# An adaLN block on one core: the causal mask as rank-32 products on row tiles, gate logits in column tiles, result gathers held apart in the plan, and order edges for the shared port

## The chip, the core and the metric

The kernel runs on one core of a Trainium2 chip. The core has TensorE (PE; its weight loads are shown apart as PEld), VectorE (DVE), ScalarE (ACT), GpSimd (POOL) and SyncE (SP), each with its own queue of instructions that runs in order, and 16 DMA engines. Matrix products go from SBUF into PSUM, whose eight banks hold 512 fp32 values in each of 128 partitions. The metric is the device time of one launch in microseconds; smaller is better.

## The reference

The input x has 32 samples of 256 tokens and 128 features. The reference computes one transformer block whose shifts, scales and gates come from a conditioning vector c of each sample:

```
mod = silu(c) @ wmod                 # sa, ca, ga, sb, cb, gb of each sample
h = layernorm(x) * (1 + ca) + sa
x = x + ga * gated_linear_attention(h)        # 4 heads, chunks of 64 tokens, running state
h = layernorm(x) * (1 + cb) + sb
x = x + gb * ffn(h)
```

The part called ffn is itself an attention and a mixture of experts:

```
h = h + mla(rmsnorm(h))              # 16 heads of 8, keys and values from a latent of 64, rope,
                                     # causal mask, softmax, over the 256 tokens of a sample
logits = rmsnorm(h) @ gate_w.T + gate_b
e = argmax(logits)                   # one of 4 experts for each token
y = relu(rmsnorm(h) @ W1[e].T + b1[e]) @ W2[e].T + b2[e]
```

Its result is h + y.

## The kernel before

The work is done in 16 steps of two samples each, that is 512 tokens, or four tiles of 128 (`NT`). A step has four parts. `gla` is the gated linear attention. `front` makes queries, keys and values of the second attention. `core` is that attention itself. `gated` is the last norm and the choice of an expert. For steps 0 to 13, `route` then sorts the tokens by expert within groups of 3, 3, 3, 3 and 2 steps: rows are scattered into a table in DRAM (line 1366), `experts` fetches blocks of 128 rows of one expert, gathers that expert's weights (line 1381), computes the two products (lines 1397 and 1411) and stores the results (line 1419). `finish` gathers the results back, four gathers of 128 rows each step (line 1431), scales and adds them, and stores the output (line 1437). Steps 14 and 15 are not sorted: `dense` computes all four experts (lines 1274 and 1285) and keeps the chosen one.

**The order of instructions** is made by a planner in the kernel's own Python, the class `Plan`. The code above records operations, each with a key that says where in the whole it belongs. `Plan.run` is a list scheduler: it has a clock for each engine, takes a cost for each operation from `weigh` (or from a figure given with `together`), and takes the operation that can start first, within a window of 1.5 steps of keys. `either` records one operation with two or three engines to choose from. Operations of one `together` stay side by side. POOL operations, and DVE operations with two operands in SBUF or in a fast mode, are marked as users of a port that both engines share (`way[4]`, from `port`); the planner lets them not overlap, through the variable `shared`. `emit` then issues the instructions in the planned order. Planned times are not kept on the chip: an engine goes on as soon as its next instruction's inputs and buffers are there.

**Buffers.** PSUM is split into one tile of four banks (`sc`), used for scores, and four of one bank (`ps`). There is only one `sc`, so each use of it waits until the one before has been read out.

**Scores are computed twice in `core`.** `masked_scores` computes scores with queries in partitions, for the row maxima: for each of two samples three sets, one with four heads a bank and 128 keys, and two with two heads a bank and 256 keys, 96 sets in all. In each, every bank gets the causal mask first, by a full-array bf16 product of the identity with a mask of 0 and -2^120 (line 1025; four products of 512 or of 256 columns), and then the scores are added in 32-row tiles of the array (line 1032). DVE reduces the four banks to negated maxima (`nm`, line 1038). `probabilities` computes the scores again with keys in partitions, with the maxima put in by products with `sel` on 8 rows of each row tile (line 1076, bf16) and the scores in 32-row tiles (line 1082). ACT takes the exponential into `pT` (line 1088), POOL sets the masked part to zero (line 1091), and `values` multiplies by the values in 32-column tiles (line 1108).

**The gate** in `gated` multiplies four fp32 tiles of 128 tokens, as weights of the array, by a matrix of four columns (line 1193), and adds the bias on DVE (line 1198).

## Time and profile before

| | |
|---|---|
| median of 9 runs | 1179.47 us (1172.43 to 1184.82) |
| profiled execution, its own time | 1178.97 us |
| its span, first to last instruction | 1176.4 us |
| granted TensorE clock, mean | 0.962 |
| line 1025, mask products | 384, busy 73.5 us |
| line 1038, maxima on DVE | 96, busy 219.7 us |
| line 1193, gate products | 128, busy 16.1 us |
| line 1431, result gathers on POOL | 56, busy 56.7 us |

The profile is of one execution, which took 1178.97 us; its rows add up to its span of 1176.4 us. Busy time of an engine is the union of its instructions. TensorE's instructions overlap and their ends are modelled, so what a block of products costs is read from its first start to the start of the next block. The chain that ended last goes back from the last instruction, at each step to what released it or to the instruction before it on its engine, so its shares say where time would have to be saved. "Another core or an unknown queue", and "remote" in the timeline, mean that a wait ended with an event that the profile does not place. A fp32 product shows as two instructions.

### The profile page before, as it was taken

What the parts mean: (1) busy time and instruction counts of PE and PEld (TensorE: products, weight loads), DVE (VectorE), ACT (ScalarE), POOL (GpSimd) and SP (SyncE); (2) the same over time, 40 slices, a digit from 0 to 9 for tenths busy, and PEclk for the clock granted to TensorE, in tenths of its full rate; (3) what the DMA queues carried; (4) which work ended last, traced back from release to release, by engine and by line L of the source; (5) the groups of instructions that cost most, each with busy time, mean ns of one, the idle gap of its engine ahead of it and who ended that gap; (6) DMA issues with size and microseconds to landing.
All of it is one profiled execution on the core that took longest, in us unless ns stands there. A gap on an engine that the chain in (4) does not pass through costs nothing.

```text
span 1176.4 us, 27631 instructions
## 1 busy us (share of the span) xinstructions
PE 1038.1 (88%) x11109; PEld 685.2 (58%) x11109; DVE 839.5 (71%) x1888; ACT 749.0 (64%) x1522; POOL 522.5 (44%) x539
## 2 busy tenths in 40 slices
PE   4778889899979999988999989799899999878995
PEld 2444555555546666665666565366666666556774
DVE  4678688878968678686888787587878678633333
ACT  3766867676766777676685858377675757443441
POOL 7123324234464343766443554634254765422422
PEclk9789999999989999999999999999999999998998
DMA  4410011001122232233322232323422334334421
GB/s 122 120 36 10 15 37 35 24 20 32 35 82 65 87 97 87 86 104 93 104 69 70 91 116 80 85 96 88 151 69 89 107 100 135 91 93 142 149 67 48
DMA packets 76608, 94.96 MB, mean 81 GB/s; under 512 B 8560, under 2 KB 59552, under 8 KB 76224
## 3 DMA queue, kind: packets, MB, share of 16 engines
q0 software_dynamic: 15456, 52.44, 14.5%
q1 hardware_dynamic: 60416, 40.10, 11.6%
q8 instruction: 87, 1.43, 0.5%
q10 hardware_dynamic: 608, 0.66, 0.2%
q14 instruction: 41, 0.34, 0.1%
HBM read 74.94 MB, written 20.59 MB: 81 GB/s over the span
## 4 chain that ended last, share of the span: by engine, by line
PE 62%; DVE 16%; ACT 7%; issue 4%; POOL 2%; another core or an unknown queue 2%; DMA 1%; DVEq 0%; POOLq 0%; ACTq 0%
PE s L1032 8%; DVE nm L1038 8%; PE ao L1108 7%; PE t L1082 6%; PE s L1025 5%; PE y L1411 4%; PE h L1397 4%; ACT pT L1088 3%; PE o L880 2%; PE t L1076 2%; PE y L1285 2%; PE wo L908 2%; PE fo L1147 2%; PE h L1274 2%
## 5 line engine op out<-in xcount | busy, mean ns | idle before, releaser
L1038 DVE TENSOR_REDUCE nm<-s 128x8 f32<-128x2048 f32 (+1 forms) x96 | 219.7, 2289 | 58.4 <-PE s L1032 52.5
L1091 POOL TENSOR_SCALAR_AFFINE_SELECT pT<-pT 128x1024 f32<-128x1024 f32 (+1 forms) x96 | 135.7, 1413 | 215.7 <-ACT pT L1088 213.0
L1088 ACT ACTIVATE pT<-t 128x2048 f32<-128x2048 f32 x96 | 180.0, 1875 | 51.3 <-PE t L1082 47.7
L1381 POOL DMA_INDIRECT w<-wtab,widx x71 | 69.5, 978 | 176.3 <-DVE y L1416 54.2
L1032 PE MATMUL s<-akT,qm 32*128 32x256 f32 (+1 forms) x2048 | 118.5, 352 | 1.9 <-issue 1.7
L1108 PE MATMUL ao<-pT,vm 128*32 128x256 f32 (+1 forms) x2048 | 104.8, 332 | 8.2 <-issue 7.2
L1082 PE MATMUL t<-qm,akT 32*128 32x512 f32 x768 | 103.8, 612 | 0.5 <-issue 0.5
L1032 PEld LDWEIGHTS s<-akT,qm 32*128 32x128 f32 x2048 | 82.4, 190 | 33.0 <-issue 26.5
L1108 PEld LDWEIGHTS ao<-pT,vm 128*32 128x32 f32 x2048 | 59.8, 110 | 68.6 <-issue 36.7
L1406 ACT ACTIVATE ht<-h,w 128x128 f32<-128x128 f32 x183 | 57.2, 366 | 64.7 <-PE h L1397 38.1
L1025 PE MATMUL s<-mask,identb 128*128 128x256 bf16 (+1 forms) x384 | 73.5, 315 | 25.1 <-DVE nm L1038 23.1
L1397 PE MATMUL h<-xT,w 128*128 128x128 f32 x568 | 82.6, 293 | 9.6 <-ACT xT L1393 8.5
L1397 PEld LDWEIGHTS h<-xT,w 128*128 128x128 f32 x568 | 73.5, 201 | 21.5 <-ACT xT L1393 10.3
L1411 PE MATMUL y<-w,ht 128*128 128x128 f32 x568 | 80.2, 286 | 6.5 <-ACT ht L1406 5.6
L1411 PEld LDWEIGHTS y<-w,ht 128*128 128x128 f32 x568 | 70.3, 193 | 23.6 <-ACT ht L1406 10.7
L1025 PEld LDWEIGHTS <-identb 128*128 128x128 bf16 x384 | 37.0, 100 | 56.6 <-issue 44.9
L1431 POOL DMA_INDIRECT res<-ys,yidx x56 | 56.7, 1012 | 26.0 <-issue 15.1
L1366 POOL DMA_INDIRECT xs<-xm,yidx x56 | 58.2, 1040 | 11.5 <-issue 8.0
L1076 PE MATMUL t<-nmT,sel 8*128 8x256 bf16 (+1 forms) x1024 | 38.7, 245 | 15.1 <-ACT pT L1088 5.7
L868 POOL TENSOR_SCALAR_AFFINE_SELECT am<-am 128x2048 f32<-128x2048 f32 x16 | 32.2, 2011 | 42.5 <-ACT am L867 42.4
L1407 DVE TENSOR_SCALAR ht<-h,w 128x128 f32<-128x128 f32 x101 | 32.6, 346 | 25.5 <-PE h L1397 12.9
L1416 DVE TENSOR_TENSOR y<-y,w 128x128 f32<-128x128 f32 x71 | 20.3, 285 | 32.5 <-PE y L1411 21.2
(272 smaller groups left out, 2308.0 us busy)
## 6 DMA issues: line engine op xcount, KB each, us to landing
xb<-xs SPq DMA_DIRECT2D x71, 64.0 KB
ys<-y SPq DMA_DIRECT2D x71, 64.0 KB
x<-in_x SPq DMA_DIRECT2D x16, 256.0 KB
mod_b<-mod_d SPq DMA_DIRECT2D x16, 256.0 KB
mod_g<-mod_d SPq DMA_DIRECT2D x30, 128.0 KB
kept<-base SPq DMA_DIRECT2D x14, 256.0 KB
back<-kept SPq DMA_DIRECT2D x14, 256.0 KB
out<-res SPq DMA_DIRECT2D x14, 256.0 KB
```

What stands on the lines that cost most here:

```text
L1025: R.tensor.matmul(last, lhsT=identb, rhs=bc(mask, 1, per), start=True, stop=False, skip_group_check=True,)
L1032: R.tensor.matmul(banks[:, g, j * n_k * P : (j + 1) * n_k * P], lhsT=qm[r, j0 + j, t0 + qb * P : t0 + (qb + 1) * P], rhs=kT[r, t0 : t0 + n ...
L1038: R.vector.tensor_reduce(nm[b][:, qb, :, j0 : j0 + per], banks.rearrange("p g (a k) -> p g a k", a=per), AX.X, ALU.max, negate=True,)
L1076: R.tensor.matmul(banks[:, g, j * nq : (j + 1) * nq], lhsT=sel[r, j0 + j, :], rhs=nmT[r, q0:L], start=(j == 0), stop=False, skip_group_che ...
L1082: R.tensor.matmul(banks[:, g], lhsT=kT[r, t0 + kb * P : t0 + (kb + 1) * P], rhs=qm[r, j0 : j0 + per, t0 + q0 : t0 + L], start=False, stop= ...
L1088: R.scalar.activation(pT, banks, AF.Exp, scale=AD ** -0.5)
L1091: R.gpsimd.affine_select(part, part, [[0, 4 * per], [1, P]], ALU.is_ge, 0.0, base=0, channel_multiplier=-1)
L1108: R.tensor.matmul(o[32 * g : 32 * g + 32, h * L + q0 : (h + 1) * L], lhsT=vm[:, 2 * b + kb, hd, :], rhs=rhs, start=(h == 0 and kb == 0 and ...
L1366: indirect(lambda idx, src, pause: scatter(xs, idx, src, pause, puts), (idx, src, pause), (idx, src, *was), (t, pause), 3000,)
L1381: indirect(lambda w, idx: take(w, wtab, idx), (w, idx), (idx, *table), (w,), 4500)
L1397: R.tensor.matmul(h_ps[:, c * P : (c + 1) * P], lhsT=w[:, c * P : (c + 1) * P], rhs=xT, start=True, stop=True,)
L1411: R.tensor.matmul(y_ps[:, 0:P], lhsT=ht[:, c], rhs=w[:, FF + c * P : FF + (c + 1) * P], start=(c == 0), stop=(c == FC - 1),)
```

## The change

- **Mask.** The four full-array products of a set become sixteen of rank 32: the mask is kept as four blocks of 32 keys by 128 queries in each group of 32 partitions, and each block is multiplied by a 32x32 part of the identity, which writes 32 key columns of each head. Four row tiles write four banks side by side. The mask is now filled on POOL and not cast from a loaded constant.
- **Gate logits.** The gate matrix, padded to 32 columns, becomes the array's weights, and the four tiles of tokens go through four column tiles; the result is copied to SBUF, transposed on TensorE, and the bias is added from a strided view.
- **Planner.** Result gathers (`R.apart = 4000`) may start in the plan only 4 us after the one before. A POOL operation that is planned within 400 ns (`TURN`) of the last DVE user of the shared port gets a wait for that DVE instruction (`behind`, `add_manual_dep` in `emit`). Costs are changed: ACT with an accumulated output, `tensor_scalar` on POOL, `mm`, and three `together` figures. `normalise` no longer offers POOL.
- **Constants.** Two constants that served the mask or nothing are not loaded, and an unused mask is not computed. An unused helper, `urgent`, is gone (not shown below).

```diff
--- before.py
+++ after.py
@@ -98,7 +98,7 @@
 class Op:
     def __init__(self, key):
         self.key, self.ways, self.deps, self.helds, self.after = key, [], set(), [], []
-        self.soon = False
+        self.soon, self.apart, self.behind = False, 0, None
 
 
 class Hand:
@@ -120,7 +120,7 @@
         self.nc, self.tc, self.kinds = nc, tc, kinds
         self.ops, self.key, self.step = [], 0.0, 0.0
         self.joined = self.choice = None
-        self.soon = False
+        self.soon, self.apart = False, 0
         self.also = [], []
         self.tensor = Hand(self, "PE", nc.tensor)
         self.vector = Hand(self, "DVE", nc.vector)
@@ -130,6 +130,7 @@
 
     WAIT = {"PE": 300, "DVE": 300, "ACT": 300, "POOL": 0, "SP": 0}
     GAIN = 1.0
+    TURN = 400
 
     def at(self, start, span, ops):
 
@@ -233,9 +234,10 @@
         if engine == "PE":
             return 0, 170
         if engine == "ACT":
-            return 190 + n * 0.815 + 80 * pointers, 0
+            more = 190 if kw.get("accum_out") is not None else 0
+            return 190 + n * 0.815 + 80 * (pointers - (more > 0)) + more, 0
         if engine == "POOL":
-            return 190 + n * (0.9 if name == "affine_select" else 2.1), 0
+            return 190 + n * {"affine_select": 0.9, "tensor_scalar": 5.2}.get(name, 2.1), 0
         inside = any(
             isinstance(v, View) and v.held.kind in ("ps", "sc") for v in (*args, *kw.values())
         )
@@ -248,7 +250,7 @@
 
     def new(self):
         op = Op(self.key)
-        op.soon = self.soon
+        op.soon, op.apart = self.soon, self.apart
         self.key += self.step
         self.ops.append(op)
         return op
...
@@ -280,7 +275,8 @@
 
     def run(self, window):
         engines = {e: 0.0 for e in ENGINES}
-        shared = 0.0
+        shared = last = 0.0
+        holder = None
         nc, ops = self.nc, self.ops
         for n, op in enumerate(ops):
             op.n = n
@@ -342,6 +338,8 @@
                     t = max(engines[e], slot)
                     if way[4]:
                         t = max(t, shared - (150 if e == "DVE" else 0))
+                    if op.apart:
+                        t = max(t, last + op.apart)
                     for d in op.deps:
                         alike = d.engine == e and (e == "PE" or not d.land)
                         t = max(t, d.freed if alike else d.end + 60)
@@ -362,6 +360,13 @@
             engines[e] = t + way[1]
             if way[4]:
                 shared = max(shared, op.freed)
+
+                if e == "DVE":
+                    holder = op
+                elif holder is not None and holder.freed > t - self.TURN:
+                    op.behind, holder = holder, None
+            if op.apart:
+                last = t
             op.way = way
             order.append(op)
             done.add(op)
@@ -395,7 +400,12 @@
                         pool, full, *_ = self.kinds[h.kind]
                         h.real = pool.tile(list(full), F32, tag=h.kind, name=h.name)
                 with self.nc.source_location(__file__, line):
-                    call(*(now(x) for x in args), **{k: now(x) for k, x in kw.items()})
+                    op.made = call(*(now(x) for x in args), **{k: now(x) for k, x in kw.items()})
+            if op.behind is not None and op.behind not in op.deps:
+                self.tc.add_manual_dep(
+                    op.made.ins, op.behind.made.ins.name,
+                    mybir.DependencyInfo(mybir.DependencyClass.Sync, mybir.DependencyReason.SCHED_ONLY),
+                )
 
 
 def bc(ap, at, n):
@@ -445,11 +455,11 @@
     cT = load("cT", [P, B], R.sync, -9.0)
     R.at(-8.9, 0.02, 1)
     R.scalar.dma_start(wmod[:, 0 : 2 * P], d["wmod"][:, 0 : 2 * P])
-    cs = keep([P, 1028], "w_consts")
-    ident, bd, tri = cs[:, 0:128], cs[:, 128:384], cs[:, 384:512]
-    cos, sin, jm = cs[:, 512:768], cs[:, 768:1024], cs[:, 1024:1028]
+    cs = keep([P, 644], "w_consts")
+    ident = cs[:, 0:128]
+    cos, sin, jm = cs[:, 128:384], cs[:, 384:640], cs[:, 640:644]
     for at, end, src, key, eng in (
-        (0, 128, 0, -8.8, R.gpsimd), (128, 512, 512, -7.0, R.gpsimd), (512, 1028, 1408, -4.0, R.sync)
+        (0, 128, 0, -8.8, R.gpsimd), (128, 644, 1408, -4.0, R.sync)
     ):
         R.at(key, 0.0, 1)
         eng.dma_start(cs[:, at:end], d["consts"][:, src : src + end - at])
@@ -482,7 +492,10 @@
     for k in range(2):
         R.gpsimd.dma_start(f_wk[k * LAT : (k + 1) * LAT, :], d["f_wk"][:, k, :])
         R.gpsimd.dma_start(f_wv[k * LAT : (k + 1) * LAT, :], d["f_wv"])
-    gw = load("gw", [P, NE], R.gpsimd, -3.0)
+    R.at(-3.0, 0.001, 1)
+    gw = keep([P, 32], "w_gw")
+    R.gpsimd.memset(gw, 0.0)
+    R.gpsimd.dma_start(gw[:, 0:NE], d["gw"])
     R.at(-3.0, 0.0, 1)
     gbb = keep([P, NE], "gbb")
     R.gpsimd.dma_start(gbb, d["gb"].partition_broadcast(P))
@@ -521,12 +534,6 @@
     eps6 = filled([P, 1], "eps6", 1e-6, -9.0)
     one = filled([P, 1], "one", 1.0, -9.0)
 
-    cmask = keep([P, P], "cmask")
-    R.at(-6.9, 0.001, 1)
-    R.vector.tensor_scalar(cmask, tri, 0.0, None, ALU.is_ge)
-    R.vector.tensor_sub(cmask, cmask, ident)
-    R.vector.tensor_scalar(cmask, cmask, -1.0, 1.0, ALU.mult, ALU.add)
-
     headsum = keep([P, P], "headsum")
     R.at(-5.5, 0.001, 1)
     R.gpsimd.memset(headsum, 0.0)
@@ -549,8 +556,14 @@
     R.at(-4.0, 0.001, 1)
     identb = keep([P, P], "identb", BF16)
     R.vector.tensor_copy(identb, ident)
-    mask = keep([P, P], "mask", BF16)
-    R.vector.tensor_copy(mask, tri)
+
+
+    mask = filled([P, 4, P], "mask", 0.0, -3.5, BF16)
+    for g in range(4):
+        part = mask[g * 32 : g * 32 + 32]
+        R.gpsimd.affine_select(
+            part, part, [[-32, 4], [1, P]], ALU.is_ge, NEG, base=0, channel_multiplier=-1
+        )
 
     R.at(-3.5, 0.001, 1)
     selc = keep([P, 4], "selc")
@@ -582,7 +595,7 @@
 
 
     def mm(n, cols):
-        return n * (2 * max(112, 0.85 * cols) + 8)
+        return n * (2 * max(116, 0.88 * cols) + 8)
 
     def mm4(n, cols):
         return n * 2 * max(140, 1.04 * cols)
@@ -616,8 +629,6 @@
             with R.either():
                 R.vector.tensor_scalar(to, of, mean, rs, ALU.subtract, ALU.mult)
                 R.scalar.activation(to, of, AF.Identity, bias=nb[:, i : i + 1], scale=rs)
-                if times == 1:
-                    R.gpsimd.tensor_scalar(to, of, mean, rs, ALU.subtract, ALU.mult)
 
     def rms_normalise(dst, src, name):
         sq = R.tile("small", [P, P], f"sq{name}")
@@ -872,7 +883,7 @@
         oT = [R.tile("mid", [P, T], f"oT{s}_{c}") for c in range(2)]
         for c in range(2):
             o = ps(f"o{s}_{c}")
-            with R.together(1.05 * mm(6, P)):
+            with R.together(1.15 * mm(6, P)):
                 for n in range(NT):
                     b, i = n // 2, n % 2
                     for k in range(2):
@@ -1018,14 +1029,18 @@
 
             n_k, t0 = qb + 1, b * L
             banks = sc(f"s{s}_{b}{qb}{j0}")
-            with R.together(mm4(per, n_k * P) + mmb(4, per * P)):
-
-                for g in range(4):
-                    last = banks[:, g].rearrange("p (a c k) -> p a c k", a=per, c=n_k)[:, :, qb, :]
-                    R.tensor.matmul(
-                        last, lhsT=identb, rhs=bc(mask, 1, per), start=True, stop=False,
-                        skip_group_check=True,
-                    )
+            with R.together(mm4(per, n_k * P) + 16 * (3 + 4 * per)):
+
+
+                for c in range(4):
+                    for g in range(4):
+                        r = slice(g * 32, g * 32 + 32)
+                        last = banks[:, g].rearrange("p (a c k) -> p a c k", a=per, c=n_k)
+                        R.tensor.matmul(
+                            last[:, :, qb, c * 32 : c * 32 + 32], lhsT=mask[r, c, :],
+                            rhs=bc(identb[r, r], 1, per), start=(c == 0), stop=False,
+                            skip_group_check=True,
+                        )
                 for j in range(per):
                     for g in range(4):
                         r = slice(g * 32, g * 32 + 32)
@@ -1187,16 +1202,24 @@
         with R.either():
             R.scalar.activation(xT, pt, AF.Copy, scale=n2w)
             R.vector.tensor_scalar(xT, pt, n2w, None, ALU.mult)
-        g_ps = ps(f"gate{s}")
-        with R.together(mm(4, NE)):
+
+        t_ps = ps(f"gt{s}")[:, 0:P]
+        with R.together(280):
             for i in range(NT):
                 R.tensor.matmul(
-                    g_ps[:, i * NE : (i + 1) * NE], lhsT=xT[:, i * P : (i + 1) * P], rhs=gw,
+                    t_ps[32 * i : 32 * i + 32, :], lhsT=gw, rhs=xT[:, i * P : (i + 1) * P],
                     start=True, stop=True,
                 )
+        gt = R.tile("small", [P, P], f"gt{s}")
+        with R.either():
+            R.scalar.copy(gt, t_ps)
+            R.vector.tensor_copy(gt, t_ps)
+        g_ps = ps(f"gate{s}")[:, 0:P]
+        with R.together(130):
+            R.tensor.transpose(g_ps, gt, ident)
         lg = R.tile("tiny", [P, NT, NE], f"lg{s}")
         R.vector.tensor_add(
-            lg, g_ps[:, 0 : NT * NE].rearrange("p (i e) -> p i e", i=NT), bc(gbb, 1, NT)
+            lg, g_ps.rearrange("p (i e) -> p i e", i=NT)[:, :, 0:NE], bc(gbb, 1, NT)
         )
         mx = R.tile("tiny", [P, NT], f"mx{s}")
         R.vector.tensor_reduce(mx, lg, AX.X, ALU.max)
@@ -1307,9 +1330,10 @@
         for was in puts:
             tc.declare_no_dep(now.ins, was.ins, reason="places differ")
         puts.append(now)
+        return now
 
     def take(out, table, idx):
-        nc.gpsimd.indirect_dma_start(
+        return nc.gpsimd.indirect_dma_start(
             out=out, out_offset=None, in_=table[:],
             in_offset=bass.IndirectOffsetOnAxis(ap=idx, axis=0),
         )
@@ -1385,7 +1409,7 @@
             with R.with_tokens(reads=g["filled"], writes=(t,)):
                 R.sync.dma_start(x, g["rows"]["xs"][b * P : (b + 1) * P, :])
             pt = ps(f"xt{s}_{b}")
-            with R.together(110):
+            with R.together(180):
                 R.tensor.transpose(pt[:, 0:P], x, ident)
             xT = R.tile("small", [P, P], f"xT{s}_{b}")
             with R.either():
@@ -1426,11 +1450,13 @@
         with R.with_tokens(reads=(state[s]["keeps"],)):
             R.sync.dma_start(base.rearrange("p i f -> p (i f)"), state[s]["kept"])
         res = R.tile("mid", [P, NT, P], f"res{s}")
+        R.apart = 4000
         for i in range(NT):
             at, row = g["yidx"][:, s - g["first"], i : i + 1], res[:, i, :]
             indirect(
                 lambda row, at: take(row, g["ys"], at), (row, at), (at, *g["stored"]), (row,), 3500
             )
+        R.apart = 0
         resv = res.rearrange("p (b i) f -> p b i f", b=2)
         mul(resv, resv, bc(gb, 2, 2))
         add(res, res, base)
```

More of the change, by code (lines that the diff above doesn't have):

```diff
@@ L266, in urgent @@
     @contextmanager
-    def urgent(self):
-        self.soon = True
-        yield
-        self.soon = False
-    @contextmanager
     def either(self):
```

## The prediction

> **What bounds the kernel now.** I read the page's totals first, then the chain that ended last, then groups with shapes kept apart, TensorE's timeline, and the timeline around the longest holes of the chain.
>
> ```profile
> span 1176.4 us, 27631 instructions
> PE 1038.1 (88%) x11109; PEld 685.2 (58%) x11109; DVE 839.5 (71%) x1888; ACT 749.0 (64%) x1522; POOL 522.5 (44%) x539
> PE 62%; DVE 16%; ACT 7%; issue 4%; POOL 2%; another core or an unknown queue 2%; DMA 1%; DVEq 0%; POOLq 0%; ACTq 0%
> PE s L1032 8%; DVE nm L1038 8%; PE ao L1108 7%; PE t L1082 6%; PE s L1025 5%; PE y L1411 4%; PE h L1397 4%; ACT pT L1088 3%; PE o L880 2%; PE t L1076 2%; PE y L1285 2%; PE wo L908 2%; PE fo L1147 2%; PE h L1274 2%
> ```
>
> TensorE is busy for 88% and carries 62% of the chain; DVE comes next with 16%, half of it the reduction nm, which frees the single four-bank score tile. So work taken off TensorE should count, if nothing else takes its place. The windows show the middle (busy us of PE, PEld, DVE, ACT, POOL, then granted clock):
>
> ```profile
> 400.00:500.00 100.00, 96.37 (x1126) 65.00 (x1125) 75.28 (x185) 73.57 (x147) 47.66 (x48) 1.00 0.28 88
> 541.00:565.00 24.00, 20.41 (x178) 14.06 (x171) 15.72 (x33) 11.91 (x26) 20.49 (x20) 0.79 0.36 95
> ```
>
> From 400 to 500 TensorE is the limit (96 of 100 us). Around 541, where twelve gathers of line 1431 stand almost back to back, its clock falls to 0.79. Now the blocks that the change rewrites, in TensorE's timeline (start, length, xcount):
>
> ```profile
> 235.14 0.40 PE L1076 MATMUL t<-nmT,sel 8*128 8x128 bf16 x16
> 235.38 1.08 PE L1082 MATMUL t<-qm,akT 32*128 32x512 f32 x8
> 249.54 1.02 PE L1025 MATMUL s<-mask,identb 128*128 128x512 bf16 x4
> 250.50 1.17 PE L1032 MATMUL s<-akT,qm 32*128 32x128 f32 x32
> 258.95 0.60 PE L1025 MATMUL s<-mask,identb 128*128 128x256 bf16 x4
> 259.48 1.15 PE L1032 MATMUL s<-akT,qm 32*128 32x256 f32 x16
> ```
>
> From the start of one block to the start of the next is what TensorE pays. The medians over the run: mask with 512 columns 957 ns, with 256 columns 528 ns; sixteen products on four row tiles with 128 columns each (line 1076, the nearest thing to the new mask) 234 ns.
>
> The last reading is the holes, first in the chain, then in the timeline at the end of the second one:
>
> ```profile
> 1115.95 4.31 another core or an unknown queue
> 1145.83 9.53 another core or an unknown queue
> ```
> ```profile
> 1150.70 0.95 POOL L1431 DMA_INDIRECT res<-ys,yidx  x1 [0.30 <-issue]
> 1151.96 0.94 POOL L1431 DMA_INDIRECT res<-ys,yidx  x1 [0.30 <-issue]
> 1155.34 0.69 DVE L1290 TENSOR_TENSOR ye<-y,b 128x512 f32<-128x512 f32 x1 [9.51 <-remote]
> 1155.38 1.84 ACT L1279 ACTIVATE ht<-h,w_cols 128x512 f32<-128x512 f32 x3 [9.82 <-remote]
> ```
>
> DVE and ACT both stop for over 9 us with their inputs ready, while POOL issues gathers, and both go on soon after the last. All five packs of result gathers (from 541, 745, 933, 1107 and 1138 us) have such a hole within or just after them. What it waits for the profile doesn't name.
>
> **The change part by part.**
>
> *Mask.* Each of 96 score sets loses four full-array products and gains sixteen of rank 32. Removed: 32 x 957 + 64 x 528 ns = 64.4 us, of which the chain holds 4.6%, 54 us; the rest lies under waits for the score tile. Added, 512-column sets: sixteen products of 128 columns, as line 1076, 234 ns. The 256-column sets: sixteen of 64 columns, not in the trace: between half of that (117, if columns rule) and all of it (234, if the instruction rules); no row is nearer to one end, so I take 175. Added: 32 x 234 + 64 x 175 = 18.7 us, saving 45.7 (41.9 to 49.5). On the chain: 54 x 45.7/64.4 = 38.3 us.
>
> [...] Line 1076 starts sixteen in 234 ns, 14.6 ns apart. [...]
>
> *Gate logits.* Sixteen blocks of 914 ns (median, line 1193) go. In their place come four fp32 products in four column tiles, 128 columns, eight instructions: line 1108 with 128 columns runs sixteen such in 551 ns, so 276; then a transpose, a quarter of line 637's 437 to 530, about 120. TensorE saves 519 ns x 16 = 8.3 us; the chain's pieces at line 1193 sum to 9.9 us, so 5.6 there. Added: one 128x128 copy out of PSUM, 0.34 to 0.37 us as lines 1392 and 1393, 16 x 0.35 = 5.6 us on ACT or DVE, and a second bank for a moment. Ranks aren't needed until a group ends, and the last dense step has its choice at 1132 and uses it at 1142; without that cover it would be about 1 us once.
>
> *What of the 43.9 us stays.* What is late next is the score tile: the 2.29 us reduction and two handovers between sets remain, and TensorE already waits 23.1 us for it in total at line 1025. But the mask is itself part of that cycle, so the cycle shortens too. Ends: half stays (22), or all (44); TensorE's 92 to 96% in most of the middle is nearer to all, so three quarters: 33 us.
>
> *Gathers.* Their start in the plan is held 4 us apart; nothing on the chip holds them, only what the plan puts between them in POOL's queue. In the middle POOL has 356 other instructions in 1176 us, one each 3.3 us, many waiting for ACT, so the spread is real there. The holes, with what the granted clock in the windows around them takes: at 552.8, 2.4 us, and a clock of 0.79 over 24 us (5.0); at 758 to 761, 2.0, and 0.84 over 21 (3.4); at 952.6, 3.6; at 1116, 4.3, and 0.91 over 18 (1.6): 22.3 us. Ends 0 and 22.3; I take half, 11, as line 1366's scatters and line 1381's weight gathers stay as dense. The pack of 1138 has almost nothing else on POOL: I leave its 12.9 us (9.5, and 0.86 over 24) as they are. And 12 gathers 4 us apart take 44 us where dense work ends 33 us after the first: in the plan three of them come after the last product of acc on POOL (1171.5 in the trace), and in its in-order queue they would wait for that: three issues of 1.25, 2.5 to landing from the last, 1.4 for product and sum, against the one sum now: about +6, half as likely as not, +3. On SP the stores of line 1437 wait for these rows; loads of x and of expert rows stand behind them there. Net -8.
>
> *Order edges.* A POOL instruction planned within 400 ns of a DVE one that uses the shared port now waits for it. Behind it in POOL's queue stand the selects on pT and am (PE waits at lines 1108 and 880), scatters and gathers. Gain: DVE's sum at line 643 takes 1237 ns in the mean for sig and 690 to 693 where undisturbed; over lines 643, 648 and 773 I count some 24 us of such stretching, at DVE's 16% of the chain 4 us. Loss: nothing where POOL's idle 56% takes it; 10 us if an eighth of the 112 selects (14) pass one DVE sum of 0.7 us on to TensorE. Between -4 and +10 I take 0.
>
> *The rest.* 25 normalisations (0.85 us) leave POOL for DVE or ACT at 0.36 to 0.48, some 10 us over two engines with room. Unloaded constants and three mask instructions of 0.2 us on DVE at 8 us lie under the wait for the modulation weights (to 9.7 us); the new mask's fills on POOL, five instructions of at most 1 us each by line 868's rate, come before 84 us, when line 1025 first runs, and after them POOL is free. All zero. Other costs of the planner only reorder.
>
> Sum: -33 - 8 = -41 us. The profiled execution took 1178.97 us (span 1176.4 and 2.6 around it), 0.5 below the median 1179.47: 1138.
>
> **The rivals.**
>
> 1. *All of it counts.* TensorE's 44 us, 22 of holes and 8 of the last pack's 12.9: 1179 - 74 = 1105. For it: 88% busy. Against: 38% of the chain is not PE.
> 2. *Spread on paper only.* POOL runs ahead of the plan, packs stay, the last three gathers come late: 1179 - 33 + 6 = 1152. For it: no wait enforces the 4 us.
> 3. *The score tile takes over.* Reduction and exponential (2.29 and 1.88 us) set the pace; half of the 44, the gathers late: 1179 - 22 + 6 = 1163. For it: nm is 8% of the chain; against: DVE has a quarter free.
> 4. *Slower: edges hold the selects.* A select that waits for a DVE stuck behind a reduction passes 2.29 us to line 1108. It decides from 41/2.29 = 18 of 112 selects on; at 27 it gives 1200. For it: POOL's order is now tied to a DVE running late at places; against: POOL is 2% of the chain.
> 5. *No difference*, 1179: products that don't overlap at 64 columns.
>
> **How the numbers follow.** Forecast 0.43 (1122 to 1150), rival 1 0.16, 2 0.17, 3 0.11, 4 0.09, 5 0.04. A measurement here tells about 0.5%, 6 us. Faster: 0.87; same 0.04; slower 0.09. From 1100 to 1170 leaves out rivals 4, 5 and a third of rival 1, 0.18: low end from full gains (1097), high end from rival 3 with some edges.
>
> **What would show it.** Right: mask blocks of about 230 and 180 ns to the next start, TensorE's busy time near 985 us, gate blocks under 0.4 us; PE still first in the chain; clock above 0.8 where the result gathers run. [...]

## The result and the profile after

The changed kernel took 1204.64 us (median of 20 runs, 1196.41 to 1212.19) against 1178.04 for the kernel before (62 runs): a ratio of 1.0226, 95% interval 1.0205 to 1.0247. It is slower by 27 us, where 41 us less was forecast. The profiled execution took 1199.23 us.

The page of the changed kernel, its span, totals and the group of the new mask (line, engine, operation, tiles, count | busy, mean ns | idle before, by whom ended):

```profile
span 1197.0 us, 30027 instructions
PE 1008.7 (84%) x12277; PEld 671.6 (56%) x12277; DVE 842.1 (70%) x1907; ACT 758.1 (63%) x1548; POOL 491.2 (41%) x511
L1039 PE MATMUL s<-identb,mask 32*128 32x64 bf16 (+1 forms) x1536 | 35.0, 204 | 46.3 <-DVE nm L1053 40.1
```

TensorE's busy time fell by 29.4 us (from 1038.1), but the span grew by 20.6, so TensorE's idle time (span less busy) grew by 50: from 138.3 to 188.3. The waits of TensorE in the changed kernel (us in total, times, longest) say part of it; the first was 23.1 us before:

```profile
PE s L1039 <- DVE nm L1053: 40.1, 30, 6.2
PE t L1091 <- DVE nm L1053: 11.7, 10, 1.8
...
PE s L1047 <- issue: 8.0, 24, 0.9
...
PE s L1039 <- issue: 6.1, 9, 1.3
```

Two things are new: a wait of 6.2 us for the reduction nm (it takes 2.29 us, and the longest wait for it was 2.4 before), and 14.1 us of waits put down to nothing (issue) inside the blocks of the mask and the scores, where lines 1025 and 1032 had 2.2 before. A place that shows the second, in the timeline of the changed kernel (start, length, engine, line, operation; in brackets the idle time before it and what ended it):

```profile
551.35 0.98 POOL L1456 DMA_INDIRECT res<-ys,yidx  x1 [1.95 <-DVE qm L979]
552.65 0.96 POOL L1405 DMA_INDIRECT w<-wtab,widx  x1 [0.32 <-DVE y L1440]
553.91 0.95 POOL L1456 DMA_INDIRECT res<-ys,yidx  x1 [0.30 <-issue]
555.16 0.95 POOL L1456 DMA_INDIRECT res<-ys,yidx  x1 [0.30 <-issue]
556.42 0.95 POOL L1456 DMA_INDIRECT res<-ys,yidx  x1 [0.30 <-issue]
...
555.02 0.34 PE L1039 MATMUL s<-identb,mask 32*128 32x128 bf16 x9
555.65 0.28 PE L1039 MATMUL s<-identb,mask 32*128 32x128 bf16 x5 [0.29 <-issue]
557.07 0.23 PE L1039 MATMUL s<-identb,mask 32*128 32x128 bf16 x2 [1.14 <-issue]
...
558.56 0.01 DVE L1133 LOAD_MASK_SELECT sums<-ao  x1 [3.51 <-remote]
558.56 0.73 DVE L1133 STREAM_SHUFFLE sums<-ao 128x512 f32<-128x512 f32 x1
558.63 0.67 ACT L1016 COPY vm<-v 128x256 f32<-128x256 f32 x2 [5.96 <-remote]
```

From 555.05 to 558.56 DVE, ACT and TensorE stand still or crawl together, with their inputs ready (ACT's 5.96 us begin with 2.4 us of ordinary waiting for a product that ends at 555.1). I call this a stop. The wait of 6.2 us has one too: at 980.6 us DVE stops for 4.2 us ahead of nm, in a pack of four indirect DMAs, while ACT goes on, and TensorE waits for it from 980.9. (A pack is a row of indirect DMAs that POOL issues one straight after the other.) Sixteen products that elsewhere take 0.23 us to the next block take over 2 us here. The result gathers, meant to be 4 us apart, run 1.25 us apart. The windows of the changed kernel (length, busy of PE, PEld, DVE, ACT, POOL, then granted clock) show that the clock got better around one pack of gathers (0.79 before, over the same window) and worse around another (1.00 before, from 933 to 956):

```profile
541.00:565.00 24.00, 21.64 (x241) 14.48 (x238) 15.86 (x37) 14.19 (x26) 10.37 (x11) 0.93 0.30 87
975.00:990.00 15.00, 8.77 (x137) 7.13 (x127) 8.79 (x15) 7.74 (x33) 7.09 (x7) 0.76 0.47 131
```

Over the run, time at less than 0.9 of the clock rose from 92.5 to 158.7 us (the records of both profiles are at 1.0 or at 0.5, so I call it half clock too; the last of the profile's clock records runs 2 to 3 us past the span in both). The last reading is POOL's timeline at the end:

```profile
1177.72 1.42 POOL L658 TENSOR_TENSOR ye<-ye,oh 128x512 f32<-128x512 f32 x1 [13.11 <-DVE ye L1313]
1180.36 0.96 POOL L658 TENSOR_TENSOR acc<-acc,mod_g 128x256 f32<-128x256 f32 x1 [1.23 <-DVE acc L654]
1181.48 0.98 POOL L1456 DMA_INDIRECT res<-ys,yidx  x1 [0.16 <-issue]
...
1189.24 0.95 POOL L1456 DMA_INDIRECT res<-ys,yidx  x1 [0.30 <-issue]
```

Seven of the last twelve gathers stand behind the last product of acc. Dense work is done by 1182; the span ends at 1197.0. So several things that speak against the forecast are there: gathers 1.25 us apart, gathers after the last acc, and longer waits for nm.

### The profile page after: what moved, and what is told of

Its sections match the earlier page's. It is cut to its first block, busy times and chain, and to the rows that moved or that the text cites. A ratio compares the mean times of both kernels' runs of the same rounds, so it can differ in the third digit from the quotient of the medians.

```text
span 1197.0 us, 30027 instructions
## 1 busy us (share of the span) xinstructions
PE 1008.7 (84%) x12277; PEld 671.6 (56%) x12277; DVE 842.1 (70%) x1907; ACT 758.1 (63%) x1548; POOL 491.2 (41%) x511
## 5 line engine op out<-in xcount | busy, mean ns | idle before, releaser
L1047 PE MATMUL s<-akT,qm 32*128 32x256 f32 (+1 forms) x2048 | 127.1, 360 | 8.4 <-issue 8.0
L1123 PE MATMUL ao<-pT,vm 128*32 128x256 f32 (+1 forms) x2048 | 97.6, 332 | 5.9 <-DVE y L1440 2.4
L1047 PEld LDWEIGHTS s<-akT,qm 32*128 32x128 f32 x2048 | 89.5, 202 | 16.0 <-issue 13.2
L1421 PE MATMUL h<-xT,w 128*128 128x128 f32 x568 | 85.5, 299 | 10.4 <-DVE xT L1416 3.9
L1421 PEld LDWEIGHTS h<-xT,w 128*128 128x128 f32 x568 | 76.4, 208 | 23.6 <-issue 7.0
L1039 PE MATMUL s<-identb,mask 32*128 32x64 bf16 (+1 forms) x1536 | 35.0, 204 | 46.3 <-DVE nm L1053 40.1
L1431 DVE TENSOR_SCALAR ht<-h,w 128x128 f32<-128x128 f32 x112 | 36.3, 347 | 52.6 <-PE h L1421 23.3
L1039 PEld LDWEIGHTS <-mask 32*128 32x128 bf16 x1536 | 22.6, 94 | 85.3 <-issue 70.8
L913 DVE SCALAR_TENSOR_TENSOR oT<-o,w_cols,ro 128x512 f32<-128x512 f32 x32 | 23.9, 746 | 32.4 <-ACT ro L912 29.7
L653 POOL TENSOR_TENSOR sig<-sig,glow 128x512 f32<-128x512 f32 x12 | 15.2, 1270 | 75.4 <-ACT sig L861 47.6
```

Source lines behind the costliest of these rows:

```text
L1039: R.tensor.matmul(last[:, :, qb, c * 32 : c * 32 + 32], lhsT=mask[r, c, :], rhs=bc(identb[r, r], 1, per), start=(c == 0), stop=False, skip ...
L1047: R.tensor.matmul(banks[:, g, j * n_k * P : (j + 1) * n_k * P], lhsT=qm[r, j0 + j, t0 + qb * P : t0 + (qb + 1) * P], rhs=kT[r, t0 : t0 + n ...
L1123: R.tensor.matmul(o[32 * g : 32 * g + 32, h * L + q0 : (h + 1) * L], lhsT=vm[:, 2 * b + kb, hd, :], rhs=rhs, start=(h == 0 and kb == 0 and ...
L1421: R.tensor.matmul(h_ps[:, c * P : (c + 1) * P], lhsT=w[:, c * P : (c + 1) * P], rhs=xT, start=True, stop=True,)
```

## The experiments

Every comparison ran on one chip, but they were not all the same chip: I call that of the result A, those of the first and second comparison B and C, that of the third and fourth D. The kernel before took 1178.04 us on A, 1140.79 on B, 1144.13 on C, 1178.39 and 1175.79 on D. Traces of A and D have stops, mostly at the same places for the same kernel: of those of the changed kernel on A, its trace on D lacks the ones that end at 785 and 1137 us and some of DVE's. No trace of B or C has one. Nothing here tells whether A and D are one chip, nor parts the chip from the time of a comparison; D showed stops in both of its comparisons. Ratios are always to the kernel before in the same comparison; a ratio can differ by some tenths of a per cent from that of the two medians (e13: 0.9897, and 1167.87/1175.79 is 0.9933). Stops are counted as idle stretches over 0.7 us of ACT and of DVE, added up, for which the profile names nothing but "remote". So a stop of both counts twice, and ordinary waiting ahead of a stop is in it, as the 2.4 us above.

| kernel (all but the ratio in us) | chip | ratio | span | TensorE busy | idle | clock < 0.9 | stops |
|---|---|---|---|---|---|---|---|
| before | A | 1 | 1176.4 | 1038.1 | 138.3 | 92.5 | 68.5 |
| after | A | 1.0226 | 1197.0 | 1008.7 | 188.3 | 158.7 | 66.8 |
| e3, order of before | B | 1.0012 | 1144.6 | 1028.1 | 116.5 | 88.4 | 0 |
| e1, mask in it | B | 0.9736 | 1109.6 | 974.2 | 135.4 | 68.9 | 0 |
| e5, after | C | 0.9936 | 1131.1 | 973.0 | 158.1 | 101.1 | 0 |
| e8, mask and gate, new plan | C | 1.012 | 1154.6 | 990.2 | 164.4 | 122.4 | 0 |
| e9, after | D | 1.0162 | 1194.1 | 1005.6 | 188.5 | 156.7 | 44.8 |
| e13, mask, old order | D | 0.9897 | 1169.1 | 1011.8 | 157.3 | 129.1 | 64.8 |
| e12, the same with edges | D | 0.981 | 1147.4 | 999.2 | 148.2 | 98.6 | 62.5 |
| e16, before, new plan | D | 1.023 | 1208.0 | 1046.4 | 161.7 | 116.1 | 61.4 |
| e14, after with pauses | D | 1.0215 | 1206.3 | 1004.5 | 201.8 | 164.0 | 2.6 |

**First: which part? (chip B)**

e1: the mask's products of the change in the kernel before; the planner is told the old figure, so every other instruction keeps its place on its engine.

```diff
             with R.together(mm4(per, n_k * P) + mmb(4, per * P)):
-                for g in range(4):
-                    ... lhsT=identb, rhs=bc(mask, 1, per) ...
+                for c in range(4):
+                    for g in range(4):
+                        ... lhsT=mask[r, c, :], rhs=bc(identb[r, r], 1, per) ...
```

> The kernel before with one thing changed: the mask of the first scores as sixteen rank-32 products a set. The planner still charges the old figure, so every engine's order is that of before; TensorE has some 45 us less work. Three theories. Score tile: what TensorE saves at the mask turns into waiting for nm and into half clock, since everything else keeps its pace; 1170 to 1182 us. Order: the mask is worth what it was priced at (33 us) and the loss of the whole change comes from the new plan; 1140 to 1155 us. Order edges: as the order theory for this run, since it has no edges.

Measured: 1112.32 us, 0.9736 (0.9678 to 0.9795). As a ratio this is the order theory's range (1140 to 1155 us are 0.968 to 0.980 of A's 1178). The groups of e3's mask (first fence, the old products) and of e1's (second), shapes apart:

```profile
L1036 PE MATMUL s<-mask,identb 128*128 128x256 bf16 x256 | 39.3, 277 | 16.7 <-DVE nm L1049 16.3
L1036 PE MATMUL s<-mask,identb 128*128 128x512 bf16 x128 | 34.2, 391 | 1.5 <-ACT pT L1099 1.1 <-DVE nm L1049 0.4
```
```profile
L1040 PE MATMUL s<-identb,mask 32*128 32x64 bf16 x1024 | 19.1, 191 | 25.2 <-DVE nm L1054 24.9
L1040 PE MATMUL s<-identb,mask 32*128 32x128 bf16 x512 | 13.5, 225 | 2.8 <-DVE nm L1054 1.7 <-ACT pT L1104 1.1
```

The kernel before has no trace on B; e3 (below) has its order, and took 1.0012 of its time, so it stands in for it. TensorE's busy time falls by 53.9 us, the span by 35.0; 18.9 come back as idle time, 9.9 of them as waits for nm in these groups (26.6 against 16.7). e3's profiled execution was its slowest, 4 us over its median, so 35.0 is a little high. So the mask does what was forecast, when nothing else moves.

e2 and e3: the order edges alone, taken from the changed kernel in e2 (its order kept), and added by the same rule to the kernel before in e3 (about a hundred waits in its order).

```diff
-            if op.behind is not None and op.behind not in op.deps:
-                self.tc.add_manual_dep(
-                    op.made.ins, op.behind.made.ins.name, ...)
```

> The changed kernel in its own order, without the waits of POOL instructions for DVE instructions (about 100 of them). Order edges theory: these hold POOL's selects and gathers behind a late DVE and cost 20 us or more; 1175 to 1185 us. Score tile and order theories: they lie in POOL's idle time; 1198 to 1208 us.

> The kernel before in its own order, with such waits added by the same rule (about 100). Order edges theory: 1195 to 1205 us. The other two: within 6 us of before, 1172 to 1184 us.

Measured: e2 1.0046 (1.001 to 1.0081), e3 1.0012 (0.9984 to 1.0041). The edges cost nothing in the old order. e2's ratio lies where the edges theory had it (1175 to 1185 us were 0.997 to 1.006 of 1178), far below the 1.0226 of A. That this is the chip and not the edges shows only in e5 below: with the edges, the changed kernel took 0.9936 on C, where there are no stops either, so without them it is no faster. With that, edges that hold POOL are out as the cause.

e4: the changed kernel without the 4 us, planned anew.

```diff
-        R.apart = 4000
+        R.apart = 0
```

> The changed kernel with the result gathers planned without the 4 us between them (a new plan). If the spread makes the end later (three gathers behind the last dense product) or blocks POOL, this is 8 to 20 us faster than the changed kernel, 1184 to 1196 us. Score tile theory: within 6 us of the changed kernel. Order theory: any plan may come out some 1% to either side, so 1190 to 1215 us.

Measured: 0.9937 (0.9903 to 0.9971). That is a little faster than before, below every range I gave, which were all taken from A. Beside e5's 0.9936 (on C) it makes no difference.

**Second: the changed kernel elsewhere, and its tail (chip C)**

e5 is the changed kernel unaltered; e6 has neither the 4 us nor the edges; e7 keeps the 4 us for the first three groups only:

```diff
-        R.apart = 4000
+        R.apart = 4000 if g["first"] < GROUPS[0] * 3 else 0
```

e8 is the kernel before with the mask, its new figure, and the gate, planned anew with the old costs, without 4 us and edges.

> The changed kernel itself, beside the same runs of before as the three below, since chips differ: before took 1178 us on the first and 1141 us on the second. If the order edges cost what the first comparison made of them (1.0226 against 1.0046 without them), 1.5% or more above before. If that difference was the chip's (the first one has holes of several us in which ACT and DVE stand still, the second has none), 0.3 to 1.0% above before.

> The changed kernel planned without the 4 us between result gathers and without the waits for DVE. It has the order of the run without the 4 us (0.994 of before) on every engine. Edges theory: 0.975 to 0.985 of before, near the mask alone in the old order (0.974). Order theory (new costs make a worse order, edges are harmless as they were in the order of before): 0.990 to 0.997.

> The changed kernel with the 4 us between result gathers kept for the first three groups and dropped for the last two, whose gathers fall into the end. The order up to there is the changed kernel's. Theory of the end: the seven gathers that stand behind the last product of acc on POOL go back in front of it, 12 to 15 us (1.0 to 1.3%) below the changed kernel of this call. Rival (the spread costs in the middle, by what it does to POOL's queue): within 5 us of the changed kernel.

> The kernel before with the new mask at its new cost and the gate in column tiles, planned anew with the other costs of before, POOL still offered to the norm, no 4 us, no edges. Order theory (the other new costs make the worse order): 0.965 to 0.977 of before. If any new plan loses what the mask wins, or the gate's longer chain costs: 0.985 to 1.000.

Measured: e5 0.9936 (0.991 to 0.9961), e6 0.9995 (0.9965 to 1.0024), e7 0.9828 (0.9776 to 0.9881), e8 1.012 (1.0048 to 1.0191). e7 fell where the theory of the end had it; e5, e6 and e8 missed every range that I gave, e5 on the fast side, e6 (by a little) and e8 on the slow one. Three things follow. The sign of the change differs from chip to chip: the same kernel is 2.3% slower on A and 0.6% faster on C. The late gathers at the end cost 1.1% here (e5 against e7). And e8, which has both saving parts and neither the 4 us nor the edges, is slower than before. The same place in e5's timeline as shown above for A:

```profile
540.03 0.98 POOL L1456 DMA_INDIRECT res<-ys,yidx  x1 [1.95 <-DVE qm L979]
541.33 0.95 POOL L1405 DMA_INDIRECT w<-wtab,widx  x1 [0.32 <-DVE y L1440]
542.59 0.95 POOL L1456 DMA_INDIRECT res<-ys,yidx  x1 [0.30 <-issue]
543.85 0.95 POOL L1456 DMA_INDIRECT res<-ys,yidx  x1 [0.30 <-issue]
...
543.69 0.40 PE L1039 MATMUL s<-identb,mask 32*128 32x128 bf16 x16
543.93 1.11 PE L1047 MATMUL s<-akT,qm 32*128 32x128 f32 x32
...
543.79 0.67 ACT L1016 COPY vm<-v 128x256 f32<-128x256 f32 x2 [2.43 <-PE v L1004]
```

It is the same pack, 1.26 us apart, and nothing stops: the sixteen mask products come in one piece, 0.24 us to the next block, and ACT has only its ordinary wait of 2.43 us.

**Third: gate, plan, edges (chip D)**

e9 is the changed kernel once more. e10 is e1 with the new gate; the copy (on DVE) and the turn are issued where the addition of the bias stood, so all else keeps its place. e11 is e1 with the block told to the planner at its new figure, so that all is planned anew, with the old gate. e12 is e1 with the edges, in the old order.

```diff
# e11
-            with R.together(mm4(per, n_k * P) + mmb(4, per * P)):
+            with R.together(mm4(per, n_k * P) + 16 * (3 + 4 * per)):
```
```diff
# e10
+        def turn(lg, bank, bias):
+            nc.vector.tensor_copy(gt, bank[:, 0:P])
+            nc.tensor.transpose(bank[:, P : 2 * P], gt, ident.ap)
+            nc.vector.tensor_add(lg, ..., bias)
```

> The changed kernel itself, on whatever chip this is. Theory of the stops (the profiled execution of the changed kernel has stretches in which ACT, DVE and TensorE stand still together while POOL issues indirect DMAs back to back; the traces of the chips of the second and third comparison have none): the ratio to the kernel before goes with the stops. If ACT and DVE show waits without a releaser of 20 us or more in this trace, as in the profiled execution (ACT 40.0, DVE 26.8 us), the ratio is 1.015 to 1.03, with over 140 us of half clock; if they show none, it is 0.985 to 1.0, with near 110 us of half clock. Rival (the sign hangs on something else, such as the day): ratio above 1.01 without such stops, or below 1.0 with them.

> The kernel before with the new mask and the new gate, but every other instruction in the place it had before on its engine (the copy of the logits and the turn are issued where their addition stood; the copy is on DVE). Theory of the plan (the new order, not the gate, gives back what the mask wins): 0.970 to 0.980, as the mask alone did in the old order (0.974). Rival (the gate's longer chain of product, copy, turn and sum costs the time): each of 16 gates then costs up to some 2 us, so 0.985 to 1.005.

> The kernel before with the new mask alone, its block told to the planner at the new figure, so that everything is planned anew; the old gate, no 4 us, no order edges, the old costs of all else. Theory of the plan: a new plan alone loses 1 to 4% against the mask in the old order (0.974), so 0.985 to 1.015, near the 1.012 of the same with the gate. Rival (the gate): about 0.974.

> The new mask in the order of before, with the order edges by the rule of the change (about 100 POOL instructions wait for a VectorE one). If the edges keep POOL off VectorE's port, as they seemed to in the changed kernel's own order (0.6 to 1.1% there): 0.963 to 0.970. If they only repair a plan that is wrong about when the two engines meet, they bring nothing in an order that was measured good: 0.972 to 0.977. If they hold POOL: above 0.98.

Measured: e9 1.0162 (1.0114 to 1.021), with stops and 156.7 us of low clock; e10 0.9972 (0.9939 to 1.0004); e11 1.0328 (1.0271 to 1.0384); e12 0.981 (0.9773 to 0.9847). e11 has the mask alone, as e13 below, which keeps the old order on the same chip and took 0.9897. Their pages (e11 first: span, totals, and the group of the mask) show the same number of TensorE's instructions:

```profile
span 1199.7 us, 29927 instructions
PE 1019.0 (85%) x12261; PEld 686.0 (57%) x12261; DVE 831.7 (69%) x1868; ACT 753.4 (63%) x1526; POOL 540.2 (45%) x559
L1031 PE MATMUL s<-identb,mask 32*128 32x64 bf16 (+1 forms) x1536 | 34.9, 202 | 46.5 <-DVE nm L1045 41.4
```
```profile
span 1169.1 us, 29941 instructions
PE 1011.8 (87%) x12261; PEld 682.9 (58%) x12261; DVE 839.1 (72%) x1887; ACT 748.0 (64%) x1522; POOL 527.6 (45%) x544
L1040 PE MATMUL s<-identb,mask 32*128 32x64 bf16 (+1 forms) x1536 | 33.1, 202 | 32.7 <-DVE nm L1054 30.3
```

The span of the new plan is 30.6 us longer; 23.4 of them are idle time of TensorE, and 11.1 of those are waits for nm at the mask. So without the gate a new plan alone turns the mask's gain into a loss, and a larger one than I had expected.

e10 fell in the range of the rival, that the gate's longer chain costs the time: it gives back 0.8% against e13. The view of its turned logits (idle time of the engine just before, us and times) says where:

```profile
its engine sat idle before it (us, times) until:
  DVE gt L1236: 13.1, 13
...
who waited for it (us, times):
  DVE lg L1236: 11.1, 16
  PEld gate L1236: 9.5, 9
```

The turn waits for the copy: 9.5 us in TensorE's weight loads, and 3.6 in its products, many of them the same time. DVE then stands 11.1 us for the turn. Both are there because I put copy, turn and sum straight behind each other. The changed kernel's plan leaves room (in its trace no turn waits for the copy), so e10 prices my placing as well as the gate; the gate by itself remains unpriced. But e10 has the changed kernel's mask and gate in the old order, and even so it is 1.9% faster than e9 on the same chip.

**Fourth: what sets off the stops, and what a plan is worth (chip D)**

e13 is e1, e15 is e7, on this chip. e14 is the changed kernel, order kept, with POOL clearing a scratch tile twice wherever an indirect DMA directly follows another ahead of step 14's work. e16 is the kernel before with one cost figure moved.

```diff
# e14, in emit
+                if op.gather and packed and op.key < 14.0:
+                    for _ in range(2):
+                        self.nc.gpsimd.memset(self.idle, 0.0)
```
```diff
# e16
     def mm(n, cols):
-        return n * (2 * max(112, 0.85 * cols) + 8)
+        return n * (2 * max(116, 0.88 * cols) + 8)
```

> The new mask alone in the order of before, once more, beside the others of this call. If this is a chip whose traces show the stops of ACT and DVE (they start in packs of indirect DMAs on POOL): near the 0.981 of the same with the order edges, 0.978 to 0.992; the more it lies above 0.981, the more the edges are worth there. If no stops: 0.968 to 0.980 as the first time.

> The changed kernel, same order, but wherever an indirect DMA directly followed another on POOL (59 places before the work of step 14) POOL first clears a scratch tile twice, some 2.3 us, so that they start over 3 us apart instead of 1.25. If packs of indirect DMAs set off the stops: on a chip that has them, the stops of ACT and DVE ahead of step 14 are gone (50 us of them in the changed kernel), and TensorE's half clock falls from 157 to near 115 us; the time falls by 10 to 40 us against the changed kernel (ratio 0.985 to 1.01), less what the later selects cost. Rival (the stops come from the place in the program, whatever POOL does): the same stops at the same instructions, and the time 1.02 to 1.04, since the pauses only hold POOL. On a chip without stops: 1.0 to 1.03, the cost of the pauses alone.

> The changed kernel without the 4 us in the last two groups. On a chip without stops it was 1.1% faster than the changed kernel (0.9828 against 0.9936). On one with stops the last packs bring stops of ACT and DVE of their own (9.8 us in the last pack of the kernel before), so the gain is smaller: 0 to 8 us against the changed kernel's 1.016 to 1.023, that is 1.008 to 1.023. If the tail is all that makes the changed kernel slow there, 1.00 or below.

> The kernel before with only the planner's figure for fp32 products moved (112 to 116, 0.85 to 0.88, as the change has it), so that all is planned anew and nothing else is changed: what a plan is worth by itself. Theory of the plan (the order of before is a good draw among plans that the costs can't tell apart): 1.01 to 1.04. Rival (the planner's figures are right and plans are alike): 0.99 to 1.005.

Measured: e13 0.9897 (0.9841 to 0.9954), e14 1.0215 (1.0153 to 1.0277), e15 1.0176 (1.0121 to 1.0231), e16 1.023 (1.0176 to 1.0284). e12 had landed just above the 0.98 that I gave for edges that hold POOL; e13, without edges, is slower still, so they do not hold it.

e14 is the clearest picture and half a miss. Its timeline at the same place:

```profile
562.43 0.98 POOL L1464 DMA_INDIRECT res<-ys,yidx  x1 [1.95 <-DVE qm L986]
563.42 2.40 POOL L401 MEMSET idle<- 128x1280 f32 x2
565.98 0.96 POOL L1413 DMA_INDIRECT w<-wtab,widx  x1 [0.15 <-issue]
566.93 2.41 POOL L401 MEMSET idle<- 128x1280 f32 x2
...
567.71 0.40 PE L1046 MATMUL s<-identb,mask 32*128 32x128 bf16 x16
...
567.81 0.67 ACT L1023 COPY vm<-v 128x256 f32<-128x256 f32 x2 [4.05 <-PE v L1011]
```

The stop is gone, and so are all of them ahead of step 14: 2.6 us are left, at 1027.6, beside a pack that was not broken up. So the packs set the stops off, on a chip that has them. Not every pack does: that of eight in e9, from 1124 us on, has no stop, where the same pack on A has one of 8.2 us on ACT. But the time did not fall. Steps 6, 9 and 12 (counted from 0, between the ends of line fo's products) are 4 to 7 us shorter than in e9, steps 7, 10, 11 and 13 each 2 to 5 longer, and TensorE now waits for POOL's selects (the waits of e14):

```profile
PE ao L1130 <- POOL pT L1113: 6.8, 5, 4.3
```

The half clock did not fall as expected either (164.0 us against 156.7). Step 0 is 8 us longer, with 44.4 us of half clock in it against 30.7, before the first indirect DMA (at 308.5 us) and so not from the pauses; in the rest of the run the half clock fell by 6 to 7 us. What the stops cost in time is therefore not shown by this run; only what sets them off is.

e15: at the end the packs of eleven and of twelve indirect DMAs come early again, and each has its stop; the second, in ACT's timeline of e15:

```profile
1178.04 1.84 ACT L1302 ACTIVATE ht<-h,w_cols 128x512 f32<-128x512 f32 x3 [10.86 <-remote]
```

The 10.86 us have some ordinary waiting in them. e15 and e9 can't be told apart, so what the late gathers cost on C is not gained back here; that the stops take it is the likely reason, not a shown one.

e16 is the plan by itself: one figure moved by under 4%, no instruction added or taken away apart from the planner's choices of an engine, and it is 27 us slower (2.3% of 1175.79).

## Why the prediction was wrong

**"The rest ... All zero. Other costs of the planner only reorder."** This is the step that failed. A reorder is not free: on D a new plan alone costs 2.3% (e16, 27 us of 1175.79), and with the mask told to the planner, e11 stands 4.3% above the mask in the old order (1.0328 against 0.9897). For the changed kernel's own plan the nearest pair is e9 against e10, which have the same mask and gate: 1.0162 against 0.9972, or 1.9%, some 22 us, with the spread gathers, the edges and the smaller parts of the change in it. The plan's order was an input of every term of my sum, since I took chain shares and covers from the old one. In place of zero this term should have had a range of tens of us. What makes one plan slower than another is shown only in part: longer waits for nm.

**"What of the 43.9 us stays."** The size was nearly right where it can be seen: e1 kept 35.0 of 53.9 us of busy time in its span, 65% against the three quarters I took, and 30 us of 1140.79 in its time, against 29 for the mask's part of the 33 (38.3 of 43.9). On D it kept less: 12 us (e13), or 22 with the edges (e12). On B half of what was lost (9.9 of 18.9 us) are waits for nm, which I had named; on D no run divides it.

**Mask.** Right. From first start to next start the new blocks take 234 and 126 ns (in the changed kernel's profile, medians), where I took 234 and 175, so 48.9 us are saved where I had 45.7. The products on four row tiles follow each other closely in this profile: sixteen in 126 ns are 7.9 ns apart, and the median step from one start to the next within a block is 4 ns.

**Gate logits.** Mis-sized: 426 and 164 ns per block in place of 276 and 120 (medians in the changed kernel's profile, from first start to the next block's start, less idle time between), so 914 less 590 is 324 ns, and sixteen of them save 5.2 us of TensorE where I had 8.3. Where the next block follows at once it is 356 and 115 ns, which would make 7.1 us.

**Gathers.** Both halves failed. The gain of 11 us from the stops did not come: 66.8 us of them are left of 68.5. I had read them as belonging to packs of result gathers; packs of a weight gather and three scatters set them off as well, and the packs of result gathers that were spread met weight gathers and closed up to 1.25 us. That is rival 2's mechanism: nothing on the chip holds the 4 us. At the end, seven gathers and not three stand behind the last product of acc; that costs 1.1% on C, 12 us where I had +3, and nothing measurable on D, where the early packs have stops of their own.

**Order edges.** What they are to prevent is in the trace of the kernel before: of DVE's elementwise operations on 128x512 (lines 643, 648 and 773), the 41 that overlap a POOL tensor operation take 1.32 us in the mean, the 118 others 0.69. Zero was right in the old order on B. Elsewhere there are hints of a gain larger than my -4: 0.6% between e6 and e4, and 1.1% between e2 and e5 (each pair on two chips), 0.9% between e13 and e12 (two comparisons on D, intervals that just overlap); no pair was run side by side. Rival 4, the one that ended on the slow side, fell: no run shows a cost of the edges. That the result lies on its side is luck: it came there through a mechanism that neither it nor I had priced.

**The sum.** On D: mask in the old order -1.0% and edges up to -0.9%, a new plan +2.3 to +4.3%, the tail about 0; the changed kernel's 1.6% lies within that. But these two plans are not the changed kernel's, and the gate is not in the sum, so it fits without proving the division. On C the same plan and tail leave 0.6% of gain. What stays open is why A and D cost this order about 66 us in span over C (1197.0 against 1131.1) and the order of before 32 over B (1176.4 against e3's 1144.6), though A's two traces have about the same total of stops. Half of the 66 is idle time of TensorE and half busy time, with 58 us more of low clock. Some of it is seen: stops now fall on DVE ahead of nm (TensorE's longest wait there is 6.2 us on A and D, 2.4 on C and in the kernel before) and inside TensorE's score blocks, where those of the kernel before were ACT's first of all (50.3 of 68.5 us). How much of the difference that makes, no run shows.

The mask alone in the order of before is faster than the kernel before wherever it ran, 0.9736 on B, 0.9897 on D, and 0.981 on D with the edges, and on D faster than the changed kernel too (1.0162).

## What to carry to other kernels

Where a planner writes the order, price an edit with the order held first, then price the new plan by itself, by moving one cost figure and nothing else: here the second was as large as the edit or larger. Never put a reorder down at zero because nothing in it is slow. And take a stall that the profile can't name for a matter of that one chip until another chip shows it too.

## What was not expected of the hardware

- Packs of indirect DMAs on POOL, some 1.25 us apart, stop ACT, DVE or both, and partly TensorE, on A and D: mostly by 2 to 6 us, by 9 us and more in packs of twelve (DVE's 9.5 us in the last one of the kernel before). On B and C no trace has a stop (0 in the table), with packs 1.26 us apart as well (e5). Most stops come back at the same instructions (e9 and the changed kernel on A), but not every pack has one. Started some 3.5 us apart, as in e14 on D, they leave 2.6 us of stops in its trace, beside a pack that was not broken up, where e9 has 44.8. The DMA packets do not differ in their mean over the run: those of the software queue take 178 ns on C (e5) and 181 on D (e9), those of the larger instruction queue (q8) 1.07 and 1.09 us. What the engines wait for is not shown.
- The kernel before is 3% slower on A and D than on B and C (1178.04 and 1178.39 us against 1140.79 and 1144.13).
- Low clock comes in pieces of about 3.4 us and their multiples: the clock records below 0.9 of the changed kernel on A last 3.41, 6.83, 10.24, 13.65 and 17.07 us, those of the kernel before 3.41, 6.83, 10.24 and 13.65, apart from the last record of each, which runs past the span (18.79 and 7.21).
